# A hand-ordered four-layer graph network kernel: the order of all jobs of a pair, and of the last pairs' jobs, arranged anew

## The chip, the cores and the metric

The kernel runs on one core of one Trainium2 chip. A core has a matmul engine (TensorE, PE in the profile; its weight loads are PEld), a vector engine (DVE), a scalar engine (ACT), GpSimd (POOL), and DMA queues; the kernel issues its transfers from SyncE's queue (SP). Each engine works through its own queue of instructions in the order in which they were emitted and waits where the next one's input or buffer isn't ready. The metric is the device time of one execution in microseconds; lower is better.

## The reference

The input x has 32 batch elements of 512 nodes with 64 features; adj is one 512 x 512 matrix for all. Four layers follow each other, each `x = x + layer(relu(layernorm(x)))`:

```python
# layer 0: v has row 0 set to the intervention value
for _ in range(3):
    effects = adj @ v
    h = relu(concat([v, effects], -1) @ W1.T + b1)
    v = h @ W2.T + b2
# layer 1
for i in range(2):
    z = relu((adj @ z) @ weights[i])
# layer 2: eight heads of gat_layer(x, graph, Wh[k], bh[k]), concatenated, leaky_relu, one gat_layer more, leaky_relu
def gat_layer(x, graph, W, b):
    h = x @ W
    s = einsum('bnd,bmd->bnm', h, h) * graph
    s = where(s == 0.0, -1e16, s)
    return einsum('bnm,bmd->bnd', softmax(s, axis=2), h) + b
# layer 3
h = x @ weight
e = leaky_relu(h @ a[:D] + (h @ a[D:]).T, 0.2)
return softmax(adj_with_unit_diagonal * e, axis=-1) @ h + bias
```

So each batch element needs nine score matrices of 512 x 512 in layer 2 (eight heads and the output layer) and one in layer 3, each with a masked softmax.

## The kernel before

**Pairs and units.** The 32 batch elements are worked as 16 pairs (`NPAIR`), the two elements of a pair side by side in the 128 partitions or along the free axis. The softmax work comes in units of two score matrices. A pair has eight head units: a, b, c, d for its first element (two heads each), g, h, i, j for its second. Unit f holds the output attention of layer 2 of the pair before (class `Out`), and e the attention of layer 3 of the pair before that (class `Last`). The software pipeline thus has several pairs in flight.

**The jobs of a unit.** `begin` takes the tiles. `s0` to `s3` are the scores: for head units and f the matmuls of `gram` (L422 for the product, L425 to add the mask), two PSUM tiles each; in unit e, ACT forms them (L692). `r0` to `r7` are the row maxima with the graph's factor (DVE, L443), and every second one has POOL negate two of them (L450). `x0` to `x3` are two exponentials each (ACT, L454). `nA` and `nB` take a reciprocal (DVE, L464) and four normalisations on POOL (L466). `t0` to `t3` turn the weights in 32 x 32 blocks (DVE, L472).

**The sums.** Two neighbouring units are summed together: number 0 is a with b, 1 is c with d, 3 is g with h, 4 is i with j. `vA` and `vB` (L482, PE) weigh the values, and need all four PSUM tiles of the matmul pool and all eight transposed pieces of both units; `us` copies them out (ACT, L537); `w0`, `w1` apply the head weights (PE, L516), `y0`, `y1` their bias and activation (ACT, L527); `o` is the projection (PE, L545) and `c` its sum over heads (DVE). After the second sum of an element, `f0`/`f1` give the output layer's features HH (PE and ACT), and `h0`/`h1` turn them to nodes: four turns on PE (L588), a copy on ACT to the one buffer `hn`, then sixteen transfers to the values' layout. The joint sum of e and f is number 2: `vA2`, `vB2` (L750), `eu` (ACT, L769 and L771), `er` (turns L588, the residual on DVE, and the output's transfers); then `oA` to `oC` (layer norm before layer 3), `oT`, `oW`, and `oN`, which makes layer 3's values `h3n` (L668) and issues 32 transfers.

**Keys.** `k0`, `k1`, `k3`, `k4` (PE, L798) and `Y0`, `Y1`, `Y3`, `Y4` (ACT, L808) make the left operands of the scores of two head units.

**The front of a pair.** `F0` to `F24` are the steps of the generator `front` (L327): layer norm F0 to F2 (F0 centres and squares on POOL; F1 takes the variance on DVE and its power on POOL, L272; F2 is the product `z` on DVE, L276, its row 0 on DVE, L331, and `xt + b2` on POOL, L332), F3 four turns (L304), F4 to F12 the three steps of layer 0 (F4, F7, F10 node products L324, F5, F8, F11 their sums, F6, F9, F12 the aggregation L312), F13 the residual and the load of x for a later pair, F14 to F16 the next layer norm, F17 to F20 layer 1, F21 to F23 the layer norm before the heads (with copies on POOL, L285), F24 the first element's features `ZZ` and values `ZQ`. `ZZ1` and `ZQ1` are the same for the second element. `values_of` calls `quarters` (L288), which issues sixteen transfers on SP's queue (L294).

**The buffers that couple them.** Scores have four PSUM tiles, all other matmul outputs have four. `hn`, `h3n`, `HH`, `ZZ`, `ZQ` have one buffer each (per element), `Y`, `us` and `z` a few.

**The order.** `manual_schedule` makes the order of emission the order on each engine's queue. It is written by hand into two tables. `PLACES` (L835) gives each job name a tick and a place: a unit that starts in tick t has its job run in tick t + dt, and within a tick the jobs run in the order of their places. A pair has ten ticks (`TICKS`), so in a steady pair the jobs of one tick come from units of different age. `TAIL` (L896) is a list of 160 tokens for the work past the last pair's ten ticks: e and p are the last joint sum's units, r, q and s the output attention and the two layer-3 attentions after it, T, U and E the sums, and 7 the last head unit. `at` looks both up, `place` and `place_sum` name a unit's jobs, and the loop from L957 goes over the pairs:

```python
dt, place = PLACES.get(name, (1, 0))
token = f"{owner[0]}:{name}"
if token in TAIL and (t + dt >= END or owner[0] in list("epqrsEU")):
    dt, place = END + 1 - t, TAIL.index(token)
jobs.setdefault(t + dt, []).append((place, fn))
```

In the last pair the units follow each other in ticks 0 to 7 instead of 0 to 3 and 6 to 9 (`t = base + (i if final else slot)`), so g to j start two ticks sooner there.

Of the kernel before, what the change touches and what calls it, by code (L numbers as in the profile page):

```python
# [21 lines left out]
def gnn_stack_kernel(  # L22
# [77 lines left out]
    E = mybir.EngineType  # L100
# [727 lines left out]
    for n, _ in enumerate(first):  # L828
# [4 lines left out]


    PLACES = {  # L835
        "begina": (0, 98), "s0a": (0, 99), "s1a": (0, 140), "s2a": (0, 203), "s3a": (0, 227),
        "r0a": (0, 118), "r1a": (0, 119), "r2a": (0, 142), "r3a": (0, 165), "r4a": (0, 241),
        "r5a": (0, 260), "r6a": (0, 301), "r7a": (1, 6), "x0a": (0, 237), "x1a": (0, 265), "x2a": (0, 308),
        "x3a": (1, 7), "t0a": (1, 258), "t1a": (1, 149), "t2a": (1, 186), "t3a": (1, 268), "nAa": (1, 83),
        "nBa": (1, 132), "beginb": (-1, 287), "s0b": (-1, 288), "s1b": (-1, 292), "s2b": (0, 65),  # L840
        "s3b": (0, 2), "r0b": (0, 68), "r1b": (0, 86), "r2b": (0, 92), "r3b": (0, 103), "r4b": (0, 163),
        "r5b": (0, 199), "r6b": (0, 107), "r7b": (0, 182), "x0b": (0, 139), "x1b": (0, 128),
        "x2b": (0, 229), "x3b": (0, 208), "t0b": (1, 35), "t1b": (1, 43), "t2b": (1, 45), "t3b": (1, 169),
        "nAb": (0, 212), "nBb": (0, 309), "beginc": (0, 41), "s0c": (0, 42), "s1c": (0, 52),
        "s2c": (0, 188), "s3c": (0, 172), "r0c": (0, 73), "r1c": (0, 75), "r2c": (0, 85), "r3c": (0, 150),
        "r4c": (0, 217), "r5c": (0, 271), "r6c": (0, 240), "r7c": (0, 261), "x0c": (0, 221),
        "x1c": (0, 197), "x2c": (0, 273), "x3c": (0, 269), "t0c": (1, 16), "t1c": (1, 38), "t2c": (1, 54),
        "t3c": (1, 62), "nAc": (0, 276), "nBc": (1, 29), "begind": (0, 47), "s0d": (0, 48), "s1d": (0, 72),
        "s2d": (0, 114), "s3d": (0, 175), "r0d": (0, 80), "r1d": (0, 91), "r2d": (0, 123), "r3d": (0, 131),
        "r4d": (0, 147), "r5d": (0, 179), "r6d": (0, 194), "r7d": (0, 226), "x0d": (0, 148),  # L850
        "x1d": (0, 177), "x2d": (0, 183), "x3d": (0, 234), "t0d": (0, 270), "t1d": (0, 307),
        "t2d": (0, 312), "t3d": (1, 15), "nAd": (0, 247), "nBd": (0, 282), "begine": (0, 21),
        "s0e": (0, 22), "s1e": (0, 23), "s2e": (0, 202), "s3e": (0, 95), "r0e": (0, 138), "r1e": (0, 152),
        "r2e": (0, 159), "r3e": (0, 162), "r4e": (0, 211), "r5e": (0, 230), "r6e": (0, 164),
        "r7e": (0, 181), "x0e": (0, 216), "x1e": (0, 283), "x2e": (1, 70), "x3e": (0, 290), "t0e": (1, 153),
        "t1e": (1, 173), "t2e": (1, 192), "t3e": (1, 228), "nAe": (0, 289), "nBe": (1, 141),
        "beginf": (-1, 25), "s0f": (-1, 311), "s1f": (-1, 26), "s2f": (-1, 313), "s3f": (0, 158),
        "r0f": (0, 27), "r1f": (0, 77), "r2f": (-1, 303), "r3f": (-1, 309), "r4f": (0, 37), "r5f": (0, 90),
        "r6f": (0, 215), "r7f": (0, 254), "x0f": (0, 176), "x1f": (0, 156), "x2f": (0, 280),
        "x3f": (0, 305), "t0f": (0, 274), "t1f": (0, 297), "t2f": (1, 120), "t3f": (1, 124),  # L860
        "nAf": (0, 218), "nBf": (1, 49), "beging": (-1, 299), "s0g": (-1, 300), "s1g": (0, 17),
        "s2g": (0, 109), "s3g": (0, 93), "r0g": (0, 32), "r1g": (0, 64), "r2g": (0, 88), "r3g": (0, 101),
        "r4g": (0, 178), "r5g": (0, 191), "r6g": (0, 129), "r7g": (0, 174), "x0g": (0, 71), "x1g": (0, 121),
        "x2g": (0, 210), "x3g": (0, 209), "t0g": (0, 222), "t1g": (0, 267), "t2g": (1, 61), "t3g": (1, 190),
        "nAg": (0, 220), "nBg": (0, 248), "beginh": (-1, 145), "s0h": (-1, 146), "s1h": (0, 50),
        "s2h": (0, 81), "s3h": (0, 116), "r0h": (0, 78), "r1h": (0, 94), "r2h": (0, 100), "r3h": (0, 108),
        "r4h": (0, 111), "r5h": (0, 115), "r6h": (0, 126), "r7h": (0, 130), "x0h": (0, 134),
        "x1h": (0, 171), "x2h": (0, 180), "x3h": (0, 185), "t0h": (0, 219), "t1h": (0, 296), "t2h": (1, 44),
        "t3h": (1, 87), "nAh": (0, 206), "nBh": (0, 233), "begini": (0, 0), "s0i": (0, 1), "s1i": (0, 10),
        "s2i": (0, 104), "s3i": (0, 67), "r0i": (0, 3), "r1i": (0, 9), "r2i": (0, 20), "r3i": (0, 39),  # L870
        "r4i": (0, 196), "r5i": (0, 200), "r6i": (0, 168), "r7i": (0, 170), "x0i": (0, 79), "x1i": (0, 125),
        "x2i": (0, 243), "x3i": (0, 231), "t0i": (1, 112), "t1i": (2, 89), "t2i": (1, 266), "t3i": (1, 236),
        "nAi": (0, 263), "nBi": (1, 8), "beginj": (-1, 204), "s0j": (-1, 205), "s1j": (-1, 284),
        "s2j": (0, 60), "s3j": (0, 30), "r0j": (-1, 278), "r1j": (0, 4), "r2j": (0, 51), "r3j": (0, 55),
        "r4j": (0, 214), "r5j": (0, 223), "r6j": (0, 117), "r7j": (0, 207), "x0j": (0, 58), "x1j": (0, 102),
        "x2j": (0, 225), "x3j": (0, 253), "t0j": (0, 291), "t1j": (1, 13), "t2j": (1, 96), "t3j": (1, 189),
        "nAj": (0, 262), "nBj": (0, 298), "vA0": (1, 201), "vB0": (1, 279), "us0": (2, 36), "w00": (2, 56),
        "y00": (2, 82), "w10": (2, 105), "y10": (2, 151), "k0": (-1, 242), "Y0": (-1, 259), "vA1": (1, 66),
        "vB1": (1, 306), "us1": (2, 34), "w01": (2, 76), "y01": (2, 97), "w11": (2, 106), "y11": (2, 154),
        "k1": (-1, 193), "Y1": (-1, 235), "vA2": (1, 137), "vB2": (1, 143), "vA3": (1, 110),  # L880
        "vB3": (1, 133), "us3": (1, 251), "w03": (2, 11), "y03": (2, 19), "w13": (2, 40), "y13": (2, 84),
        "k3": (-1, 224), "Y3": (-1, 238), "vA4": (1, 232), "vB4": (1, 256), "us4": (1, 293),
        "w04": (1, 310), "y04": (2, 46), "w14": (2, 53), "y14": (2, 57), "k4": (-1, 295), "Y4": (-1, 302),
        "o01": (2, 244), "c01": (2, 252), "o03": (2, 286), "c03": (3, 127), "f0": (4, 257), "h0": (5, 74),
        "o11": (2, 166), "c11": (2, 272), "o13": (2, 136), "c13": (2, 187), "f1": (3, 33), "h1": (3, 69),
        "eu": (2, 28), "er": (2, 213), "oA": (5, 285), "oB": (5, 294), "oC": (6, 31), "oT": (6, 250),
        "oW": (8, 281), "oN": (9, 12), "ZZ1": (0, 161), "ZQ1": (-1, 157), "F0": (-2, 144), "F1": (-2, 245),
        "F2": (-2, 255), "F3": (-1, 5), "F4": (-1, 155), "F5": (-1, 160), "F6": (0, 14), "F7": (0, 198),
        "F8": (0, 239), "F9": (1, 304), "F10": (2, 135), "F11": (2, 195), "F12": (3, 246), "F13": (4, 18),
        "F14": (4, 59), "F15": (4, 167), "F16": (5, 24), "F17": (5, 277), "F18": (6, 63), "F19": (7, 249),  # L890
        "F20": (7, 264), "F21": (7, 275), "F22": (8, 122), "F23": (8, 184), "F24": (9, 113),
    }

    TAIL = """  # L896
        7:t2j e:begine e:s0e p:beginf p:s2f 7:t3j e:s1e e:r0e e:r2e e:s2e p:s1f e:r4e e:r5e e:s3e T:vA4 T:vB4
        e:x2e p:s0f T:us4 T:w04 e:r6e e:r3e e:r7e p:r4f T:y04 p:r5f p:r0f p:r2f T:w14 e:x3e e:r1e p:s3f p:r3f
        e:nBe p:r1f T:y14 p:x1f p:r6f e:x0e U:f0 p:x0f T:o13 T:c13 p:r7f T:f1 p:nAf e:t3e p:x2f r:beginf r:s0f
        r:r0f r:r1f T:h1 p:x3f r:s2f p:t1f e:t2e p:nBf e:x1e r:r4f e:nAe 7:x3j r:r5f r:x0f U:h0 r:s3f p:t2f  # L900
        r:r6f r:r7f e:t0e p:t3f p:t0f r:x3f r:s1f e:t1e r:r2f r:r3f E:vA2 r:x2f E:vB2 r:x1f 7:nBj r:nBf r:nAf
        r:t0f r:t1f E:eu r:t2f r:t3f E:er E:oA E:oB r:vA5 E:oC r:vB5 r:ou E:oT r:or E:oW E:oN q:begine q:s0e
        q:s2e q:r0e q:r1e q:s1e q:r2e r:oA r:oB q:r4e q:s3e r:oC q:r3e r:oT q:r6e r:oW q:r7e q:x1e q:x0e q:r5e
        r:oN s:begine s:s0e s:s3e s:r0e q:x3e q:x2e q:nAe s:s1e s:s2e s:r1e s:r6e s:r7e s:x3e q:t1e q:nBe
        s:r2e s:r3e q:t0e s:r4e s:r5e q:t2e s:x0e s:x2e s:nBe s:x1e q:t3e s:nAe s:t2e q:vA5 q:vB5 s:t3e s:t0e
        q:lu s:t1e q:lr s:vA5 s:vB5 s:lu s:lr
    """.split()
    PER_SUM = ("us", "w0", "y0", "w1", "y1")
    jobs = {}
    LEAD, TICKS = 2, 2 * NQ + 2  # L910
    END = LEAD + TICKS * NPAIR - 2
    owner = [None]

    def at(t, name, fn):
# [126 lines left out]
```

## Time and profile before

| what | us |
|---|---|
| the three runs | 2363.77, 2368.61, 2368.47 (median 2368.47) |
| the profiled execution's own time | 2365.83 |
| its span, from the first to the last instruction | 2364.0 |
| start, 0 to 160 | 160, PE busy 120.2 |
| first steady pair's run-up, 160 to 297.15 | 137.2, PE busy 134.2 |
| 13 steady pairs, 297.15 to 2098.76 | 1801.6, PE busy 1753.0 |
| last pair, 2098.76 to 2235 | 136.2, PE busy 125.3 |
| the rest, 2235 to 2364 | 129.0, PE busy 71.4 |

Busy time of the whole span: PE 2204.1 us (93%), DVE 1880.1 (80%), ACT 1500.4 (63%), POOL 1301.3 (55%). The mean granted clock of TensorE is 0.981 of full speed. A pair's beginning is taken at the first of the four aggregations on `z` (L312). The costliest groups of instructions, with their count and mean length, are

| line, engine, operation | count | mean ns |
|---|---|---|
| L454 ACT exponential, 128x512 | 1280 | 718 |
| L466 POOL normalisation, 128x512 | 1280 | 703 |
| L472 DVE transpose, 128x1024 | 640 | 1229 |
| L443 DVE maximum, 128x512 from PSUM or SBUF | 1152 | 681 |
| L422 PE scores, 64x512 | 4096 | 603 |
| L482 PE weighted sums, 32x256 | 17152 | 374 |
| L272 POOL power, 128x8 | 64 | 1739 |

In a row of the timeline the columns are: begin in us, length, engine, line, operation, output and inputs, shapes, count, and in brackets the idle time before it and what ended that. A matmul row joins the matmuls that follow each other without a gap on one line.

### The profile page before, as it was taken

How to read it: one execution, taken by the hardware profiler on the slowest of the kernel's cores; microseconds unless marked ns; L12 is line 12 of the kernel's file. 1: busy time of each engine (PE TensorE's matmuls, PEld its weight loads, DVE VectorE, ACT ScalarE, POOL GpSimd, SP SyncE). 2: the span in 40 equal slices, each digit the busy share in tenths (PEclk: the TensorE clock that was granted, in tenths of full speed). 3: DMA queues.
4: the chain of work that ended last, by engine and by line, in shares of the span. 5: the costliest groups of instructions: out<-in, count | busy, mean ns of one | idle time of the engine just before them, and what ended most of it. 6: DMA issues, size and time to landing. Idle time of an engine off the chain costs nothing.

```text
span 2364.0 us, 81802 instructions
## 1 busy us (share of the span) xinstructions
PE 2204.1 (93%) x34507; PEld 1194.3 (51%) x34507; DVE 1880.1 (80%) x4098; ACT 1500.4 (63%) x3752; POOL 1301.3 (55%) x2163
## 2 busy tenths in 40 slices
PE   6889999999999999999999999999999999998873
PEld 3445555555555555555555555555555555554442
DVE  3668788888888888888888888878888888888754
ACT  1446557666675766767676666757666675766644
POOL 2345565645655565556566556656555655555433
PEclk9999999999999999999999999999999999999986
DMA  3101011111111111111111111111111111111112
GB/s 85 19 6 31 13 25 32 30 21 31 31 28 28 32 31 21 31 31 30 26 33 32 21 29 31 32 25 33 30 24 29 30 28 25 30 27 26 20 25 46
DMA packets 260596, 68.25 MB, mean 29 GB/s; under 512 B 257660, under 2 KB 258692, under 8 KB 260228
## 3 DMA queue, kind: packets, MB, share of 16 engines
q1 hardware_dynamic: 259424, 62.86, 15.8%
q8 instruction: 270, 4.42, 0.8%
q14 instruction: 98, 0.80, 0.1%
q10 hardware_dynamic: 804, 0.17, 0.0%
HBM read 8.40 MB, written 4.19 MB: 5 GB/s over the span
## 4 chain that ended last, share of the span: by engine, by line
PE 71%; DVE 11%; ACT 6%; POOL 5%; issue 2%; SPq 2%; DMA 2%; ACTq 0%; POOLq 0%; DVEq 0%
PE s L422 18%; PE mm L482 14%; PE mm L312 9%; PE mm L750 6%; DVE sm L472 4%; PE mm L516 4%; PE s L425 4%; DVE sm L443 4%; PE mm L545 3%; PE mm L324 3%; ACT sm L454 3%; POOL sm L466 3%; SPq L294 2%; PE mm L798 2%; PE mm L358 2%
## 5 line engine op out<-in xcount | busy, mean ns | idle before, releaser
L454 ACT ACTIVATE sm<-sm,nmx 128x512 f32<-128x512 f32 x1280 | 909.2, 718 | 184.4 <-POOL nmx L450 180.9
L466 POOL TENSOR_SCALAR sm<-sm,rs 128x512 f32<-128x512 f32 x1280 | 874.4, 703 | 213.3 <-DVE rs L464 206.5
L472 DVE STREAM_TRANSPOSE sm<-sm 128x1024 f32<-128x1024 f32 x640 | 775.2, 1229 | 92.3 <-POOL sm L466 86.1
L443 DVE CUSTOM_DVE_ANT_0 sm<-s,A 128x512 f32<-128x512 f32 x1152 | 732.5, 681 | 134.4 <-PE s L425 127.0
L422 PE MATMUL s<-ZZ,Y 64*64 64x512 f32 x4096 | 571.4, 603 | 25.7 <-ACT Y L808 18.5
L482 PE MATMUL mm<-sm,vq 32*64 32x256 f32 (+1 forms) x17152 | 487.8, 374 | 22.8 <-DVE sm L472 18.9
L450 POOL TENSOR_SCALAR nmx<-mx 128x2 f32<-128x2 f32 x640 | 147.4, 234 | 614.9 <-DVE mx L443 555.4
L482 PEld LDWEIGHTS mm<-sm,vq 32*64 32x64 f32 x17152 | 397.0, 133 | 125.4 <-issue 45.3
L422 PEld LDWEIGHTS s<-ZZ,Y 64*64 64x64 f32 x4096 | 152.7, 132 | 248.7 <-issue 119.0
L425 PE MATMUL s<-NEGM,I2b 64*64 64x512 bf16 x2304 | 261.4, 377 | 0.0
L454 ACT ACTIVATION_READ_ACCUMULATOR sm<-sm,nmx 128x1 f32 x1280 | 248.9, 194 | 0.0
L537 ACT COPY us<-mm 128x256 f32<-128x256 f32 x256 | 75.8, 378 | 166.9 <-PE mm L482 166.9
L527 ACT ACTIVATE y<-mm,cols 128x512 f32<-128x512 f32 x256 | 158.3, 689 | 30.2 <-PE mm L516 30.2
L312 PE MATMUL mm<-AT,v 128*128 128x512 f32 x384 | 173.0, 593 | 0.0
L750 PE MATMUL mm<-sm,vq 32*64 32x128 f32 (+1 forms) x5504 | 133.1, 315 | 33.7 <-issue 17.1
L425 PEld LDWEIGHTS <-I2b 64*64 64x64 bf16 x2304 | 83.1, 107 | 158.3 <-issue 157.5
L272 POOL TENSOR_TENSOR r<-ve,mhalf 128x8 f32<-128x8 f32 x64 | 111.3, 1739 | 76.7 <-DVE ve L270 61.1
L750 PEld LDWEIGHTS mm<-sm,vq 32*64 32x64 f32 x5504 | 114.0, 133 | 59.4 <-issue 30.8
L516 PE MATMUL mm<-us,Wh 64*64 64x512 f32 x1024 | 132.7, 595 | 0.7 <-ACT us L537 0.7
L545 PE MATMUL mm<-y,Wo_sb 128*64 128x512 f32 x512 | 124.5, 605 | 0.0
L312 PE MATMUL mm<-AT,z 128*128 128x512 f32 x256 | 118.8, 607 | 2.0 <-DVE z L276 1.4
L312 PEld LDWEIGHTS mm<-AT,v 128*128 128x128 f32 x384 | 73.1, 191 | 92.8 <-issue 91.2
(135 smaller groups left out, 1987.2 us busy)
## 6 DMA issues: line engine op xcount, KB each, us to landing
vq<-z SPq DMA_DIRECT2D x512, 32.0 KB, 1.9
vq<-hn SPq DMA_DIRECT2D x512, 32.0 KB, 1.9
vq<-h3n SPq DMA_DIRECT2D x512, 32.0 KB, 1.9
xt<-in_x_dram SPq DMA_DIRECT2D x32, 128.0 KB, 2.5
out_dram<-xo SPq DMA_DIRECT2D x32, 128.0 KB, 2.1
A<-in_adj_dram SPq DMA_DIRECT2D x3, 1024.0 KB
Wh<-in_L_gnn_Wh_dram SPq DMA_DIRECT2D x2, 256.0 KB
Wo_sb<-in_L_gnn_W_out_dram SPq DMA_DIRECT2D x1, 256.0 KB
```

The costliest lines, as they stand in the source:

```text
L312: nc.tensor.matmul(pe, lhsT=v[:, m].rearrange("p j d -> p (j d)"), rhs=AT[:, m, :], start=(first and m == 0), stop=(m == NT - 1),)
L422: nc.tensor.matmul(pss[half][R[ab], :], lhsT=lhsT, rhs=rhs, start=True, stop=False)
L425: nc.tensor.matmul(pss[half][R[ab], :], lhsT=I2b[R[half], :], rhs=NEGM[R[half], k, :], start=False, stop=True,)
L443: nc.vector.tensor_tensor_reduce(self.sm[:, s, :], src, graph, 1.0, -FMAX, ALU.mult, ALU.max, self.mx[:, s : s + 1])
L454: nc.scalar.activation(self.sm[:, s, :], self.sm[:, s, :], AF.Exp, bias=self.nmx[:, s : s + 1], accum_out=self.ssum[:, s : s + 1],)
L466: nc.gpsimd.tensor_scalar(self.sm[:, s, :], self.sm[:, s, :], self.rs[:, s : s + 1], 1.0, ALU.mult, ALU.mult)
L472: nc.vector.transpose(out=two, in_=two)
L482: nc.tensor.matmul(self.u[i][R[c], 0 : weights.shape[1] * 32], lhsT=values[32 * i : 32 * i + 32, jb, :], rhs=weights[32 * i : 32 * i + 32, ...
L516: nc.tensor.matmul(py[c][r, :], lhsT=Wh2[R[c], 2 * (self.q - 1 + c) + ab, r], rhs=self.us[R[c], 2 * ab : 2 * ab + 2].rearrange("p i (s e) ...
L527: nc.scalar.activation(y, py[c], AF.Prelu, bias=cols[:, h : h + 1], alpha=0.01)
L545: nc.tensor.matmul(pa[R[ab], :], lhsT=Wo_sb[:, h, :], rhs=self.y[h], start=(k == 0), stop=(k == 1),)
L750: nc.tensor.matmul(self.u[i][R[c], (s % NS) * 32 : (s + ns) * 32], lhsT=values(i)[r, jb, :], rhs=sm[r, s : s + ns, 32 * jb : 32 * jb + 32] ...
```

## The change

Only the two tables are changed. 312 of the 315 names in `PLACES` get another tick or place, and the 160 tokens of `TAIL`, the same ones, stand in another order. No job is added, taken out or altered, nor are the tiles, the buffers or the code that reads the tables. What an engine's queue holds in a pair is the same; the order differs, and for some jobs the pair period in which they run.

Cut to the entries that the prediction speaks of (each name's tick and place; the numbers are only ranks, so that two entries compare only within one table):

```diff
     PLACES = {
...
-        "s2i": (0, 104), "s3i": (0, 67), "r0i": (0, 3), "r1i": (0, 9), "r2i": (0, 20), "r3i": (0, 39),
+        "s2i": (0, 63), "s3i": (0, 68), "r0i": (0, 25), "r1i": (0, 29), "r2i": (0, 51), "r3i": (0, 56),
...
-        "k4": (-1, 295), "Y4": (-1, 302), "f0": (4, 257), "h0": (5, 74), "begini": (0, 0), "s0i": (0, 1),
+        "k4": (-1, 265), "Y4": (-1, 312), "f0": (4, 259), "h0": (5, 3), "begini": (0, 8), "s0i": (0, 9),
...
-        "t1h": (0, 296), "t2h": (1, 44), "t3h": (1, 87), "F20": (7, 264), "F21": (7, 275), "F22": (8, 122),
+        "t1h": (0, 248), "t2h": (0, 282), "t3h": (1, 59), "F20": (7, 260), "F21": (7, 292), "F22": (8, 72),
...
-        "F0": (-2, 144), "F1": (-2, 245), "F2": (-2, 255), "F3": (-1, 5), "nAi": (0, 263),
+        "F0": (-2, 84), "F1": (-2, 241), "F2": (-2, 258), "F3": (-1, 32), "nAi": (0, 249),
...
-        "us1": (2, 34), "w01": (2, 76), "y01": (2, 97), "s2f": (-1, 313), "s3f": (0, 158),
+        "us1": (1, 293), "w01": (2, 6), "y01": (2, 50), "s2f": (0, 77), "s3f": (0, 76),
...
-        "nBe": (1, 141), "r5f": (0, 90), "x2f": (0, 280), "x3f": (0, 305), "nBf": (1, 49), "t3f": (1, 124),
+        "nBe": (1, 128), "r5f": (0, 170), "x2f": (0, 250), "x3f": (0, 291), "nBf": (1, 2), "t3f": (1, 62),
...
-        "t0c": (1, 16), "t1c": (1, 38), "t2c": (1, 54), "t3c": (1, 62), "r5c": (0, 271), "r7d": (0, 226),
+        "t0c": (0, 311), "t1c": (0, 244), "t2c": (1, 160), "t3c": (1, 184), "r5c": (0, 245), "r7d": (0, 179),
...
-        "k1": (-1, 193), "Y1": (-1, 235), "o13": (2, 136), "F8": (0, 239), "t3j": (1, 189),
+        "k1": (-1, 125), "Y1": (-1, 164), "o13": (2, 185), "F8": (0, 178), "t3j": (1, 193),
...
-        "ZQ1": (-1, 157), "F24": (9, 113), "oN": (9, 12), "h1": (3, 69),
+        "ZQ1": (5, 281), "F24": (9, 209), "oN": (9, 12), "h1": (3, 48),
...
     TAIL = """
-        7:t2j e:begine e:s0e p:beginf p:s2f 7:t3j e:s1e e:r0e e:r2e e:s2e p:s1f e:r4e e:r5e e:s3e T:vA4 T:vB4
-        e:x2e p:s0f T:us4 T:w04 e:r6e e:r3e e:r7e p:r4f T:y04 p:r5f p:r0f p:r2f T:w14 e:x3e e:r1e p:s3f p:r3f
-        e:nBe p:r1f T:y14 p:x1f p:r6f e:x0e U:f0 p:x0f T:o13 T:c13 p:r7f T:f1 p:nAf e:t3e p:x2f r:beginf r:s0f
...
+        e:begine e:s0e 7:t2j e:s3e 7:t3j p:beginf p:s0f e:s2e T:vA4 e:r4e e:s1e T:vB4 p:s2f e:r5e e:r2e T:us4
+        e:r3e p:r0f e:r6e e:x1e p:r1f T:w04 e:r7e p:r4f T:y04 p:r5f p:s1f T:w14 e:r0e e:x2e p:r2f T:y14 p:s3f
+        e:r1e e:x3e e:x0e e:nBe T:o13 T:c13 p:r3f U:f0 T:f1 p:x0f e:nAe e:t2e e:t3e e:t0e T:h1 p:r6f p:x2f
...
```

In words, as they fall out on the queues of a steady pair:

- `h0` stands after `k4` and before the scores of i, instead of among them; t1 and t2 of h stand before F20's and F21's DVE instructions.
- F2 stands after i's first normalisation; before, i's came after it.
- `w01` stands right behind f's first scores, ahead of the scores s3 and s2 of f; before it stood behind s2. `us1` moves with it to the tick before.
- f's x2 stands before `eT`, and its r5 behind e's second normalisation.
- c's t1 stands before its r5 and t0, its t2 and t3 behind d's maxima; j's t3 behind F8; `k1` before `o13`.
- `ZQ1`'s sixteen transfers stood right behind F24's sixteen of the same pair, at the end of the pair period; now they stand in the next period, behind those of `h1`, of `oN` and the load of x, five ticks after the pair begins.
- In `TAIL` the sum of i and j stands right behind the first scores of e and f, and the jobs from `o13` to `h1` stand earlier.

## The prediction, on record before the changed kernel was run

> **What bounds the kernel now.** I read the page first, then the busy time in windows of one pair each, the timeline of TensorE over one pair, and the other engines' timelines wherever TensorE stood.
>
> ```profile
> span 2364.0 us, 81802 instructions
> ...
> PE   6889999999999999999999999999999999998873
> ...
> PEclk9999999999999999999999999999999999999986
> ```
>
> After a start of some 150 us the matmul engine is nine tenths busy or more at full clock; only the last 130 us are loose. A pair repeats at the line "L312 x8 on z"; the windows between two such places are these (span of the window, then PE, PEld, DVE, ACT and POOL busy, the clock, the DMA share and GB/s):
>
> ```profile
> 297.15:435.34 138.19, 134.62 (x2146) 73.19 (x2145) 116.28 (x254) 92.83 (x233) 81.13 (x134) 1.00 0.16 27
> ...
> 989.74:1128.03 138.29, 134.80 (x2146) 73.00 (x2145) 117.05 (x256) 93.61 (x235) 81.12 (x134) 1.00 0.17 29
> ...
> 2235.00:2364.00 129.00, 71.41 (x1584) 46.67 (x1584) 65.42 (x139) 59.05 (x146) 46.83 (x71) 0.75 0.19 32
> ```
>
> The mean of the 13 pairs between 297.15 and 2098.76 is 138.59 us, of which TensorE works 134.8. DVE at 117 has 21 us to spare, ACT and POOL more. No job is added or removed, so a pair can gain only what TensorE stands, 3.5 us, plus what is hidden in stretched groups. The timeline of TensorE in the pair from 989.74 shows where it stands:
>
> ```profile
> 996.78 1.09 PE L422 MATMUL s<-ZZ,Y 64*64 64x512 f32 x8 [0.69 <-ACT Y L808]
> ...
> 1013.45 0.63 PE L304 MATMUL mm<-ident,z 128*128 128x128 f32 x4 [1.02 <-DVE rs L464]
> ...
> 1093.91 1.35 PE L422 MATMUL s<-HH 64*64 64x512 f32 x6
> ...
> 1112.00 4.73 PE L750 MATMUL mm<-sm,vq 32*64 32x256 f32 x210 [0.80 <-DVE sm L472]
> ```
>
> First the scores of unit i wait for Y4; then F3's turns wait (the named reciprocal is only the last DVE event, the real supplier is z of F2 and its row 0, L331, written at 1013.09); the scores f s2 are stretched by two maxima that still hold their PSUM tiles; then the joint sum waits for the last transpose of f. The DVE and POOL timelines give the cause of the second:
>
> ```profile
> 1009.60 1.67 POOL L272 TENSOR_TENSOR r<-ve,mhalf 128x8 f32<-128x8 f32 x1
> 1011.23 1.27 POOL L332 TENSOR_TENSOR xt<-xt,b2bc 128x512 f32<-128x512 f32 x1
> ...
> 1011.30 1.75 DVE L276 SCALAR_TENSOR_TENSOR z<-xc,r 128x512 f32<-128x512 f32 x1 [1.79 <-POOL r L272]
> ```
>
> z takes 1.75 us beside POOL's xt+b2; elsewhere in this pair its shortest is 0.69.
>
> **The change part by part.** It moves the place of 312 of 315 job names and reorders the tail list. Most moves leave a job between the same neighbours on TensorE; I cost those that touch a stand or make one, with the durations above.
>
> *h0 between k4 and the scores of i.* Before, k4 (ends 996.09), Y4 on ACT (its first half ends 996.74), s0 of i. Now h0's four turns, 0.60 us in the row at 1000.70, fill 0.60 of the 0.69. The later place of h0 is emptied: i s0 to s3 follow each other, held only by DVE's maxima r0 to r3, which end at 1000.56 as before. On DVE transposes t1 and t2 of h move ahead of F20 and F21, into the 1.14 us in which DVE waited for F20, so one transpose (1.15) leaves the stretch before F22. The sum of g and h, at 1002.53 before, starts at about 1001.8, and its own stretch (7.52 against 7.09 in its other places, it waited for h t3) goes as well. Gain 0.7 to 1.1, taken 0.9.
>
> *F0 to F3.* From F22's first DVE instruction to F3 it took 10.60 us (1002.85 to 1013.45), in a chain DVE–POOL–DVE–POOL–DVE: variance, power (1.67), z, centring (1.04), square (1.04), variance, power, z. TensorE has 7.09 of sum and 2.4 of scores over it. F2 now stands behind i nA, so POOL normalises i (L466) beside z, and xt+b2 comes after it. At 1094.38 z beside L466 took 0.69; so 1.06 leaves the chain, which becomes 9.5 and just fits under 9.5. Gain 1.0; bounds 0 (z stays at 1.75) and 1.06. Row 1094.38 is the same instruction beside the same POOL instruction, so I take its price.
> The Trainium skill (SBUF — State Buffer, Who interferes with whom) speaks against this: a DVE instruction with two SBUF inputs and a GpSimd instruction that reads SBUF block each other, and the second to issue waits for the first. By it z could wait for one normalisation of 0.68, and the gain would be about 0.4, the sum some 8 us smaller; the row at 1094.38 shows no such wait.
>
> *w01 ahead of f s2.* Now TensorE meets w01 right after f s0 (ends 1093.9), and w01 needs us1, the third ACT job after e x1. In ACT's queue e x3 stands before us1, and its bias, POOL's L450, stands behind the power of F15 (it ended at 1093.44). With F15 one maximum (0.61) earlier e x3 starts at about 1092.9, us1 at 1094.3, w01 at 1095.0: a new stand of 1.1. Behind it wait f s3, f s2, w11, k3 and through them Y3. In return f s2 is no longer stretched (1.88 instead of 1.08, so 0.8). Net loss 0.3; bounds 0 (us1 as early as POOL allows) and 1.3 (us1 at 1095.12 as now).
>
> *The joint sum.* f x2 moves before eT and f r5 behind e nB's normalisation on POOL, but the last chain (f x3, f nB, 2.71 of POOL, f t3) keeps its order; worked through, f t3 ends at 1111.4 instead of 1111.95, and TensorE, 0.3 later, gets there at 1111.5. Gain 0 to 0.8, taken 0.3.
>
> *The other moves.* c t1 goes ahead of c r5 and t0, c t2 and t3 behind d's maxima, j t3 behind F8, k1 before o13. Each costs DVE, ACT or POOL the same instructions; what hides them is 7.09 of TensorE per head sum. I put them at nothing; if the cover of the c–d stretch is gone, it is the last rival below.
>
> *ZQ1.* Its 16 transfers on SP's queue move from the end of the previous pair's jobs to behind h1, oN's 32 and the load of xt. In a steady pair these are issued by 1107.1; 16 at 0.645 and 1.95 to land end at 1119.4, 21 us before the sum that reads them: nothing. In the last pair, units g to j come two ticks sooner, and there it counts:
>
> ```profile
> 2186.00 23.76 SPq L294 DMA_DIRECT2D vq<-h3n  x32
> ```
>
> By this row SP is free at 2209.8, the 13th of 16 (at 0.74, as in this row) lands at 2221, the last at 2223. That sum ran from 2215.28 and ended at 2224.0; now its first quarter runs as the pieces land and three quarters of 7.1 follow: 2228. Loss 4, and the gains of k1 and k4 in the last pair (their Y waits of 2.08 and 1.58) are lost in this stand. Bounds 0 and 8.
> The skill (TensorE: Matmul & The Clock Gate, Part 1) says that a matmul engine idle for about 3.4 us falls to half clock; by that the sum after this stand would need up to 3.5 more. In the trace the clock was 0.83 and a sum took 8.54 instead of 7.09 after stands of 2.87 and 0.98.
>
> *The tail list.* The sum of i and j now stands before f's scores s1 and s2, so it starts when j t3 is turned (2240.3) and not at 2242.35: 2 less. From its end to h1's copy I count 12.5 us in the new order, against 14.2, since two or three exponentials less stand before f1's copy on ACT. From that copy on SP sets the end (16 issues, landing, second copy, joint sum at 2277.73; then twice 32 issues), as before. Gain 3.5 against the loss of 4.
>
> Sum: 0.9 + 1.0 − 0.3 + 0.3 = 1.9, rounded to 2.0 with the small shortenings, in 14 pairs (0 to 13) is 28; 0.7 in pair 14, which has no F3; tail −0.5. From 2365.8 of the profiled execution: **2338 us**. Its time lies 2.6 below the median of the runs shown (2368.47) and within them.
>
> **The rivals.**
> *More is gained:* the stand before the joint sum (0.80+0.33+0.66) goes too and w01 does not wait: 3.7 a pair, 14 times, 52 less: 2314. For it: DVE has 21 us of slack a pair. Against: f nB's chain keeps its order.
> *The gain is eaten:* w01 waits 1.3, z stays slow and the joint sum slips by as much as TensorE came early; the order of nearly all TensorE jobs is the same, so the pair stays 138.6: 2366, between 2358 and 2371. For it: all these supplies come from queues that were on time by under 1 us.
> *Slower:* c t1 waits in DVE's queue for POOL's fourth normalisation (2.71 instead of the 1.59 that t0 waited), and c t2 and t3 (2.3) now lie behind d's maxima, before the sum of c and d. DVE would be late there by 1.1 + 2.3 = 3.4, less the 2.0 gained: 1.4 a pair, 14 times: 2386. It decides once DVE's idle time between 1065.3 and the sum at 1085.68, 2.8 us in its timeline, is used up by these; most of that idle time waits for POOL and ACT, which move too.
>
> **How the numbers follow.** Forecast 0.47 (own range 2326 to 2354), more 0.15, eaten 0.18, slower 0.20. A measurement of this kernel can tell 0.2% (4.7 us) from no change. Of "eaten", 0.06 is still faster, 0.10 within, 0.02 above. Faster 0.68, same 0.10, slower 0.22. The range 2312 to 2375 takes in the first three and leaves out most of the fourth.
>
> **What would show it.** Right: a pair of 136 to 137 us; the first scores of i within 0.2 us of h0; z in F2 near 0.7 and no stand before F3; in the last pair a stand of several us before the sum of g and h. Wrong in its step: z at 1.75; w01 standing over 1.3 us; the sum of c and d waiting for a transpose. The prediction as a whole is wrong if the pair stays above 138.

## The result and the profile after

The changed kernel takes 2348.24 us (median of four runs, 2346.53 to 2349.57) beside 2367.72 for the kernel before: a ratio of 0.9921, with a 95% interval of 0.9903 to 0.9938. The forecast was 2338 in a range of 2312 to 2375. The profiled execution took 2346.53 with a span of 2344.7, 19.3 less than before.

From the page of the changed kernel (span; then PE's busy tenths and its granted clock in 40 slices):

```profile
span 2344.7 us, 81823 instructions
...
PE   6889999999999999999999999999999999999883
...
PEclk9899999999999999999999999999999999999986
```

The windows of the changed kernel (span, then busy time of PE, PEld, DVE, ACT, POOL, the clock, DMA share and GB/s) have the start, the pair that answers to the one shown of before, all 13 steady pairs, and the rest:

```profile
160.00:301.10 141.10, 135.23 (x1894) 70.99 (x1895) 108.87 (x240) 82.53 (x211) 72.92 (x127) 0.96 0.11 19
...
985.64:1122.04 136.40, 133.19 (x2147) 71.99 (x2145) 116.53 (x256) 93.34 (x235) 81.64 (x134) 1.00 0.17 29
...
301.10:2078.71 1777.61, 1733.10 (x27874) 937.63 (x27873) 1514.03 (x3314) 1212.89 (x3041) 1061.28 (x1742) 1.00 0.17 29
...
2215.00:2344.70 129.70, 78.08 (x1601) 51.52 (x1600) 69.17 (x143) 61.87 (x154) 47.35 (x74) 0.74 0.19 32
```

A pair now takes 136.74 us instead of 138.59 (1777.61 / 13), so the 13 steady pairs give 24.0, more than the 19.3 by which the span fell. Of that 4.8 were given back: the first marker (F19's aggregation, the row "L312 on z") stands at 301.10 instead of 296.99, 4.1 later, and what follows the last marker takes 266.04 instead of 265.35, 0.7 more.

The timeline of TensorE in the pair from 985.64 has the places that were shown of before:

```profile
992.08 0.66 PE L588 MATMUL mm<-ident,HH 128*128 128x128 f32 x4
992.84 1.09 PE L422 MATMUL s<-ZZ,Y 64*64 64x512 f32 x8
...
997.98 7.16 PE L482 MATMUL mm<-sm,vq 32*64 32x256 f32 x256
...
1007.46 0.63 PE L304 MATMUL mm<-ident,z 128*128 128x128 f32 x4
...
1089.14 1.09 PE L516 MATMUL mm<-us,Wh 64*64 64x512 f32 x8 [1.30 <-ACT us L537]
...
1105.94 4.67 PE L750 MATMUL mm<-sm,vq 32*64 32x256 f32 x201 [0.28 <-DVE sm L472]
```

The first four rows have no brackets: h0's turns fill the wait for Y4, the sum of g and h runs in one piece, and F3 finds its z. The fifth is a new stand (idle time of TensorE), w01 waiting for us1. The last is the old wait before the joint sum, 0.28 instead of 0.80.

To compare kernels, the pair is cut at fixed rows of TensorE's timeline, from the beginning of one to the beginning of the next, and averaged over the 13 steady pairs of each profiled execution. Only the stretches that differ are shown; the runs are explained below.

| run | marker to sum gh | sum gh | its end to w03 (F3 within) | end of sum cd to F17 | F17 to joint sum | joint sum | whole pair | first marker at | after last marker |
|---|---|---|---|---|---|---|---|---|---|
| before | 12.95 | 7.53 | 3.95 | 7.12 | 12.08 | 9.93 | 138.59 | 297.0 | 265.4 |
| changed | 12.34 | 7.10 | 2.94 | 7.67 | 11.72 | 10.33 | 136.74 | 301.1 | 266.0 |
| F2 alone | 12.95 | 7.53 | 3.18 | 7.10 | 12.06 | 10.22 | 138.32 | 297.1 | 266.8 |
| h0 alone | 12.35 | 8.13 | 3.94 | 7.09 | 12.06 | 10.11 | 138.73 | 295.8 | 267.5 |
| h0, t1, t2 | 12.35 | 7.12 | 3.83 | 7.06 | 12.06 | 10.17 | 137.68 | 295.7 | 267.1 |
| w01 alone | 12.95 | 7.55 | 3.92 | 8.00 | 12.21 | 10.18 | 139.85 | 295.3 | 268.9 |
| list alone | 12.95 | 7.53 | 3.94 | 7.10 | 12.06 | 10.07 | 138.71 | 296.8 | 262.5 |
| four places, list | 12.35 | 7.17 | 3.04 | 7.10 | 12.06 | 10.15 | 137.13 | 295.8 | 260.8 |
| changed, w01 back | 12.34 | 7.16 | 2.93 | 8.96 | 11.71 | 10.28 | 138.08 | 300.9 | 269.3 |
| changed, ZQ1 early | 12.36 | 7.15 | 2.94 | 7.62 | 11.71 | 10.25 | 136.92 | 300.4 | 260.6 |
| changed, g t3 late | 12.34 | 7.16 | 2.93 | 7.70 | 11.71 | 10.44 | 136.96 | 298.3 | 267.3 |
| both of these | 12.36 | 7.15 | 2.94 | 7.69 | 11.71 | 10.39 | 137.04 | 297.4 | 260.1 |
| and f moved | 12.36 | 7.09 | 2.95 | 6.91 | 12.17 | 10.20 | 136.52 | 296.5 | 261.6 |

Kernels with one and the same steady order (the changed one, and those with ZQ1 or g's t3 moved) differ by up to 0.3 in the pair, so smaller differences of that column say nothing. The execution of before that was profiled took 2365.83, 2.6 below the median shown ahead (2368.47), and its joint sum is the shortest here: with the same steady order the list alone has 10.07 and a pair of 138.71.

### The profile page after: what moved, and what is told of

The parts are those of the page before. It is cut to its first block, busy times and chain, and to the rows that moved or that the text cites. A ratio compares the mean times of both kernels' runs of the same rounds, so it can differ in the third digit from the quotient of the medians.

```text
span 2344.7 us, 81823 instructions
## 1 busy us (share of the span) xinstructions
PE 2189.2 (93%) x34507; PEld 1186.5 (51%) x34507; DVE 1872.8 (80%) x4098; ACT 1496.4 (64%) x3752; POOL 1306.7 (56%) x2163
## 4 chain that ended last, share of the span: by engine, by line
PE 76%; DVE 10%; ACT 6%; POOL 3%; issue 2%; SPq 2%; DMA 1%; ACTq 0%; POOLq 0%; DVEq 0%
PE s L422 19%; PE mm L482 16%; PE mm L312 11%; PE mm L750 5%; PE mm L545 5%; PE s L425 4%; PE mm L516 4%; DVE sm L443 4%; DVE sm L472 4%; ACT sm L454 3%; PE mm L324 3%; PE mm L798 2%; SPq L294 2%; PE mm L358 2%; ACT y L527 1%
## 5 line engine op out<-in xcount | busy, mean ns | idle before, releaser
L482 PE MATMUL mm<-sm,vq 32*64 32x256 f32 (+1 forms) x17152 | 488.1, 378 | 29.8 <-DVE sm L472 20.3
L482 PEld LDWEIGHTS mm<-sm,vq 32*64 32x64 f32 x17152 | 400.3, 135 | 129.3 <-issue 56.6
L312 PE MATMUL mm<-AT,v 128*128 128x512 f32 x384 | 172.9, 593 | 0.0
L750 PE MATMUL mm<-sm,vq 32*64 32x128 f32 (+1 forms) x5504 | 131.4, 313 | 27.4 <-issue 21.5
L750 PEld LDWEIGHTS mm<-sm,vq 32*64 32x64 f32 x5504 | 111.8, 132 | 52.7 <-issue 29.4
L263 POOL TENSOR_TENSOR xc<-x,nmu 128x512 f32<-128x512 f32 x48 | 55.3, 1151 | 139.8 <-DVE nmu L261 139.8
L312 PE MATMUL mm<-AT,z 128*128 128x512 f32 x256 | 119.1, 609 | 3.8 <-DVE z L276 1.4
```

The lines of the kernel that those rows point to most:

```text
L312: nc.tensor.matmul(pe, lhsT=v[:, m].rearrange("p j d -> p (j d)"), rhs=AT[:, m, :], start=(first and m == 0), stop=(m == NT - 1),)
L482: nc.tensor.matmul(self.u[i][R[c], 0 : weights.shape[1] * 32], lhsT=values[32 * i : 32 * i + 32, jb, :], rhs=weights[32 * i : 32 * i + 32, ...
L750: nc.tensor.matmul(self.u[i][R[c], (s % NS) * 32 : (s + ns) * 32], lhsT=values(i)[r, jb, :], rhs=sm[r, s : s + ns, 32 * jb : 32 * jb + 32] ...
```

## The experiments

Each says from which of the two kernels it starts; edits are shown as entries of the tables. Ratios are to the kernel before, timed beside each of them.

### F2 alone, in the kernel before

```diff
-        "F2": (-2, 255),
+        "F2": (-2, 263.5),
```

> The kernel before with one move: F2 behind i's first normalisation, so that z lies beside POOL's normalisations and xt + b2 comes after. Theory (contention with the addition on POOL stretched z): z falls from 1.75 to about 0.7 us, the stand before F3 of 1.0 goes, 14 pairs give 14 us: about 2353.5. Rival (z waits for one normalisation of 0.68 instead): z about 1.4 with its wait, 0.4 a pair, about 2362. Rival (F3 was not what held the pair, the next supply is as late): no change, 2367.

Measured: 2362.93 us, ratio 0.9967 (0.9955 to 0.9980): half of what was expected. POOL's and DVE's timelines of this run at F2:

```profile
1009.93 3.23 POOL L466 TENSOR_SCALAR sm<-sm,rs 128x512 f32<-128x512 f32 x4
1013.13 1.28 POOL L332 TENSOR_TENSOR xt<-xt,b2bc 128x512 f32<-128x512 f32 x1
...
1009.98 0.69 DVE L276 SCALAR_TENSOR_TENSOR z<-xc,r 128x512 f32<-128x512 f32 x1 [1.72 <-POOL r L272]
1010.70 0.52 DVE L331 COPY z<-ivt 1x128 f32<-1x128 f32 x1
```

z takes 0.69 as in the theory, and the rival with z at 1.4 is out. The two engines still get in each other's way, but in other places: the four normalisations take 3.23 instead of 2.71 (the first 1.21), and the copy of row 0 behind z, which F3 needs too, is longer than in the kernel before:

```profile
1013.09 0.21 DVE L331 COPY z<-ivt 1x128 f32<-1x128 f32 x1
```

From the begin of z to the end of row 0 it takes 1.25 instead of 2.01 (means of the 13 pairs), so 0.76 leaves the chain and not 1.06, and the stretch with F3 falls by 0.77. A wait of 0.25 for row 0 remains in this pair, since F22 comes no earlier: it begins 0.33 after the sum of g and h, as in the kernel before, and 0.20 ahead of it in the changed kernel. Of the 0.77, the pair keeps 0.27; 0.20 comes back before the sum of i and j, and the joint sum is 0.29 longer.

### h0 alone, and h0 with two transposes, in the kernel before

```diff
-        "h0": (5, 74),
+        "h0": (5, -1),
```

> The kernel before with one move: h0 ahead of the scores of i. Theory: the wait for Y4 (0.69) is filled, but the sum of g and h still waits for h t3, whose DVE queue is unchanged, so that its stretch grows by what it starts earlier: 0 to 0.3 a pair, 2363 to 2368. Rival (the filler alone makes the gain that the forecast put at 0.6 of its 0.9): 0.6 a pair, 2359.

Measured: 2369.93 us, ratio 0.9998 (0.9988 to 1.0007), no change. The sum of g and h begins 0.60 earlier and takes 0.60 longer. The timeline of TensorE in that run shows what it meets:

```profile
1002.10 0.66 PE L482 MATMUL mm<-sm,vq 32*64 32x256 f32 x8
1003.16 7.14 PE L482 MATMUL mm<-sm,vq 32*64 32x256 f32 x248 [0.40 <-DVE sm L472]
```

Eight matmuls run, then the sum waits for h's last transpose: the filler moved the stand and removed nothing. The second run also puts h's t1 and t2 ahead of F20 and F21 on DVE:

```diff
-        "h0": (5, 74), "t1h": (0, 296), "t2h": (1, 44),
+        "h0": (5, -1), "t1h": (0, 263.5), "t2h": (0, 274.5),
```

> As the run with h0 ahead of the scores of i, and h's transposes t1 and t2 ahead of the DVE instructions of F20 and F21. Theory (h t3 was the limit, and comes 1.15 earlier by this): the sum of g and h starts 0.6 earlier and takes 7.09 instead of 7.52, together 1.04 a pair as in the changed kernel, 14 pairs: about 2353. Rival (the other moves of the changed kernel were needed for it): under 0.5 a pair, over 2360.

Measured: 2354.44 us, ratio 0.9931 (0.9916 to 0.9946), with 12.35 and 7.12 in the table as in the changed kernel. With no other move these three bring 1.01 of the 1.04 that the two stretches gain in the changed kernel. The filler needs the transposes; the transposes without the filler were not run.

### The list of the last pairs alone

The kernel before, with all 160 tokens of `TAIL` in the changed kernel's order:

```diff
-        7:t2j e:begine e:s0e p:beginf p:s2f 7:t3j e:s1e e:r0e e:r2e e:s2e p:s1f e:r4e e:r5e e:s3e T:vA4 T:vB4
...
+        e:begine e:s0e 7:t2j e:s3e 7:t3j p:beginf p:s0f e:s2e T:vA4 e:r4e e:s1e T:vB4 p:s2f e:r5e e:r2e T:us4
...
```

> The kernel before with the new list of the last pairs' jobs alone. Theory (the list is worth what the forecast said): 3.5 less, about 2364, all of it behind the last pair's period. Rival (SP's 64 issues of the last two groups of h3n set the end, and they start only a little earlier): under 1.5 less, 2366 to 2368.

Measured: 2364.43 us, ratio 0.9977 (0.9967 to 0.9987), 5.4 less; in the profile 262.5 after the last marker, where the kernels with the old list and the old ZQ1 have 265.4 to 268.9. By these rows the list is worth 3 to 6. The rival's limit of 1.5 less lies outside the interval, so it is out.

### ZQ1's transfers early in the changed kernel

```diff
-        "ZQ1": (5, 281),
+        "ZQ1": (0, 231),
```

The timelines of TensorE and of SP's queue in the last pair of the changed kernel show the stand that this is to remove:

```profile
2193.91 0.65 PE L482 MATMUL mm<-sm,vq 32*64 32x256 f32 x4
2195.75 0.61 PE L482 MATMUL mm<-sm,vq 32*64 32x256 f32 x2 [1.19 <-DMA vq<-z]
2198.33 8.50 PE L482 MATMUL mm<-sm,vq 32*64 32x256 f32 x250 [1.97 <-DMA vq<-z]
...
2166.15 22.30 SPq L294 DMA_DIRECT2D vq<-h3n  x32
2188.54 10.25 SPq L294 DMA_DIRECT2D vq<-z  x16
```

SP is busy with h3n until 2188.5, ZQ1's first pieces are issued then, the last at 2198.8, and the sum takes 12.85 from its first matmul to the next scores instead of 8.71 before. Part of that is the clock: the last 250 matmuls take 8.50 at a granted clock of 0.83, where 250 took 7.15 at 1.00 in the kernel before.

> The changed kernel with one move: ZQ1's sixteen transfers right behind the sum of the pair before that reads the old values, instead of behind those of h1 and oN. Theory: the waits for vq of 1.19 and 1.97 in the last pair's sum of g and h go and that sum takes 7.1 to 8 us instead of 12.85; some 4 us there, of which the later waits give back at most half: 2344 to 2346. Rival (the end is set by SP's 64 issues of the last h3n, which start when the layer norms are done whatever came before): under 1 less, 2347.5. In the steady pairs both expect nothing: 136.7.

Measured: 2342.47 us, ratio 0.9880 (0.9865 to 0.9895), clear of the changed kernel's 0.9921. The same sum in this run:

```profile
2195.69 7.66 PE L482 MATMUL mm<-sm,vq 32*64 32x256 f32 x256
```

There is no wait, and what follows the last marker is 5.4 shorter (260.6 beside 266.0). The theory let later waits give back up to half of the gain; the whole of it reached the end.

### w01 back in the changed kernel, and w01 alone in the kernel before

```diff
-        "w01": (2, 6), "y01": (2, 50),
+        "w01": (2, 77.5), "y01": (2, 78),
```

> The changed kernel with one move undone: w01 (and y01) behind f's scores s3 and s2. Theory (the stand of 1.30 before w01 is new, and the scores stretched by 0.8 were the smaller evil): 0.5 a pair less, 14 pairs 7 us: about 2341. Rival (the scores are held by their maxima as before and the joint sum waits for f's last transpose anyway): no change, 2348.

Measured: 2369.01 us, ratio 0.9994 (0.9985 to 1.0004): the whole gain is gone, and both the theory and the rival are wrong. The timelines of TensorE and ACT in this run:

```profile
1096.55 0.59 PE L516 MATMUL mm<-us,Wh 64*64 64x512 f32 x2
...
1101.02 1.55 PE L312 MATMUL mm<-AT,z 128*128 128x512 f32 x3 [0.89 <-ACT y L527]
...
1097.68 1.30 ACT L527 ACTIVATE y<-mm,cols 128x512 f32<-128x512 f32 x2 [1.13 <-PE mm L516]
1098.88 0.71 ACT L454 ACTIVATE sm<-sm,nmx 128x512 f32<-128x512 f32 x1
1099.59 0.71 ACT L454 ACTIVATE sm<-sm,nmx 128x512 f32<-128x512 f32 x1
1100.29 1.25 ACT L527 ACTIVATE y<-mm,cols 128x512 f32<-128x512 f32 x2
```

ACT stands 1.13 for w01, then does y01, f's x1 and y11; F17 waits for the PSUM tile that y11 gives back. The changed kernel has f's x1 between y01 and y11, so by these rows a late w01 delays F17 by the exponentials too. The reverse question is what w01 ahead does in the old order, where y01 and y11 are neighbours on ACT:

```diff
-        "w01": (2, 76), "s2f": (-1, 313),
+        "w01": (2, 34.5), "s2f": (0, 36),
```

> The kernel before with w01 ahead of f's scores s2 alone. Theory (w01 has to wait for us1 on ACT wherever it stands, and whatever is put behind it waits too; that undoing it in the changed kernel cost 1.3 a pair comes from y11 and f's x1 having been put around it on ACT): the stretch from the sum of c and d to F17 grows from 7.12 to between 7.6 and 8.1, of which the wait before the joint sum, 0.8, can take up to 0.8: 0 to 0.5 a pair, 2369 to 2376. Rival (w01 early is worth 1.3 a pair by itself, as its undoing cost): 2351.

Measured: 2387.77 us, ratio 1.0074 (1.0057 to 1.0091): slower, on the theory's side but by more than its 0.5 a pair. The stretch grows to 8.00, within its bounds, and the wait before the joint sum absorbs none of it (0.94 instead of 0.80). The row of w01 in this run:

```profile
1101.70 1.09 PE L516 MATMUL mm<-us,Wh 64*64 64x512 f32 x8 [1.71 <-ACT us L537]
```

So the place of w01 has no price of its own. In the old order it costs 1.26 a pair to put it early (0.88 of it in this stretch, 0.25 in a longer joint sum), in the new one 1.34 to put it late. That the order on ACT makes the difference is argued from the two traces; no run changed that order alone.

### g's t3 behind h's r3 in the changed kernel

In the start of the changed kernel, the scores before F19 wait 7.32 us (5.02 before). DVE's timeline there:

```profile
159.38 1.25 DVE L472 STREAM_TRANSPOSE sm<-sm 128x1024 f32<-128x1024 f32 x1
160.84 2.58 DVE L472 STREAM_TRANSPOSE sm<-sm 128x1024 f32<-128x1024 f32 x2 [0.21 <-POOL sm L466]
163.34 0.65 DVE L443 CUSTOM_DVE_ANT_0 sm<-s,A 128x512 f32<-128x512 f32 x1
```

The maximum that frees the scores' PSUM tile stands behind four transposes, one more than before.

```diff
-        "t3g": (1, 40),
+        "t3g": (1, 104),
```

> The changed kernel with one move undone: g's transpose t3 behind h's maximum r3. Theory (in the first pair, which has no e and f between, DVE's maxima of h stand behind two transposes that wait for POOL, the stand of 7.32 at 164 us): about 1.2 us less in the start alone, nothing in the steady pairs: 2347. Rival (the start lost its time elsewhere, to the order of i and the granted clock): no change in the start; with t3 later the sum of g and h may wait for it in every pair, 2348 to 2356.

Measured: 2349.16 us, ratio 0.9908 (0.9893 to 0.9923), not told from the changed kernel's 0.9921. In the profile the wait is 5.99 instead of 7.32 and the first marker comes at 298.3 instead of 301.1. So t3's place makes 1.3 of the 2.3 by which this wait had grown; its effect on the time of the whole is below what these runs resolve.

### Four places and the list, in the kernel before

```diff
-        "F2": (-2, 255), "h0": (5, 74), "t1h": (0, 296), "t2h": (1, 44),
+        "F2": (-2, 263.5), "h0": (5, -1), "t1h": (0, 263.5), "t2h": (0, 274.5),
```

and `TAIL` as changed.

> The kernel before with h0, h's t1 and t2, and F2 moved as in the changed kernel, and the new list of the last pairs' jobs: four places and the list, the other 308 places as they were. Theory (these carry the gain of the changed kernel): 1.0 a pair at the sum of g and h, 0.75 at F3, and 5 at the end, less 0.3 a pair of longer joint sums: a pair of 137.1 to 137.4, about 2345 in all, as fast as the changed kernel. Rival (the gains at F3 and at the sum need the reordered work of f behind them, else the joint sum waits for f's last transpose longer): the wait before the joint sum grows from 0.8 to over 1.5, a pair of 138, 2352 or more.

Measured: 2340.93 us, ratio 0.9883 (0.9868 to 0.9898), faster than the changed kernel and than expected. The pair is 137.13, and the wait before the joint sum stays as it was:

```profile
1102.43 4.74 PE L750 MATMUL mm<-sm,vq 32*64 32x256 f32 x210 [0.79 <-DVE sm L472]
```

The other 308 places bring 0.39 a pair (5.1 in 13), hardly more than the differences that say nothing, and cost 5.3 before the first marker and 5.2 behind the last. ZQ1 is one of these places, and by the run above it alone accounts for the 5.2.

### Both repairs of the changed kernel, and three moves of f

```diff
-        "ZQ1": (5, 281), "t3g": (1, 40),
+        "ZQ1": (0, 231), "t3g": (1, 104),
```

> The changed kernel with ZQ1 right behind the sum that frees its buffer and g's t3 behind h's r3, the two moves that were tried alone. Theory (one acts in the last pair, the other in the first): the gains add, 6 and 2, about 2340 beside 2348; the first pair's marker at 298.3 instead of 301.1, no wait for vq before the sum of g and h of the last pair. Rival (the start's gain is lost again before the steady pairs, as the time of the run with t3 alone may say): 2342.5.

Measured: 2338.42 us, ratio 0.9870 (0.9854 to 0.9887). The first marker is at 297.4 and what follows the last takes 260.1, as expected of each; beside the run with ZQ1 alone the intervals overlap. The next kernel moves three jobs of f besides:

```diff
-        "s3f": (0, 76), "w11": (2, 100), "y11": (2, 127), "r7f": (0, 221),
+        "s3f": (0, 5), "w11": (2, 79), "y11": (2, 80), "r7f": (0, 210),
```

> The kernel with ZQ1 and g's t3 moved, and besides: f's scores s3 ahead of w01, y11 ahead of f's exponentials x1, f's maximum r7 ahead of its first normalisation. Theory (w01 waits for us1 on ACT anyway, s3 fits into that stand of 1.30; F17 waits for y11's PSUM tile and not for matmuls; the last exponential of f waits for the negation behind POOL's normalisations): the stretch from the sum of c and d to F17 falls from 7.67 to between 6.6 and 7.1, the wait before the joint sum stays under 0.8, a pair gains 0.4 to 0.9, 6 to 12 us, some 2331. Rival (ACT has no idle time in this stretch and sets the joint sum): the stretch falls but the wait before the joint sum grows by as much, no change beside the run without these moves.

Measured: 2335.11 us (2334.17 to 2336.4), ratio 0.9858 (0.9843 to 0.9872), the fastest here; all its runs lie below all of the one before it (2337.61 to 2340.78). The gain is 3.3, not the 6 to 12 expected. The theory's first half holds: the stretch to F17 falls from 7.69 to 6.91. Of these 0.78, the next stretch takes 0.46 back, but not as the rival had it: the wait before the joint sum is gone, and the scores of g before it are slower. TensorE and DVE in this run:

```profile
1095.12 1.32 PE L422 MATMUL s<-ZZ,Y 64*64 64x512 f32 x6
...
1091.90 2.58 DVE L472 STREAM_TRANSPOSE sm<-sm 128x1024 f32<-128x1024 f32 x2 [0.45 <-POOL sm L466]
1094.40 0.65 DVE L443 CUSTOM_DVE_ANT_0 sm<-s,A 128x512 f32<-128x512 f32 x1
```

The scores need a tile that the maximum at 1094.40 frees, and this stands behind two transposes that wait for POOL's normalisation. From the end of the sum of c and d it comes 14.13 later (mean of the 13 pairs), in the changed kernel 13.87: TensorE came early, and this supply didn't.

## Why the prediction was right

The direction, the mechanism of the main gain and the range were right; the size was two thirds of the forecast (19.5 of 30 by the medians). Four places with the list, moved alone, bring as much and more, so the cause of the gain is shown. Point by point:

- **The pair:** 1.85 less, forecast 1.9 to 2.0. That it fits so well is in part luck: w01 and the joint sum fell short by 0.6 together, and h0 and the small moves, put at nothing, made up for 0.5. *h0* was put at 0.9 and measured 1.04 in the changed kernel, 1.01 with three places alone. The forecast named both halves, but its 0.6 for the filler is worth nothing without h's transposes (h0 alone: 0.9998).
- **F0 to F3** was put at 1.0 and gives 1.01 in the changed kernel, but not by z alone. z takes 0.69 as the row at 1094.38 had it, and all 14 of before that took 1.75 or more are gone (13 other products of this line now take 0.96 instead of 0.69); the copy of row 0 behind it, which the step didn't price, grew from 0.21 to 0.52, so the move itself gives 0.77, and 0.27 in the pair. With h0, t1 and t2 besides, which bring F22 forward, the stretch falls by 0.91. The Trainium skill (SBUF — State Buffer, Who interferes with whom) says that the order of issue decides who blocks. By the begins in the profile POOL was first both times: beside xt + b2, 0.07 ahead, z took 1.75, as the rule has it; beside the normalisations, 0.04 ahead, z lost nothing and POOL's four took 0.51 longer, which doesn't agree, unless the order of issue was another than these begins show.
- **w01** was put at a loss of 0.3 and lost 0.55, within its bounds, with a stand of 1.30 for the forecast's 1.1, at the edge of what it named as a sign of being wrong. The step priced TensorE's order and ACT's up to us1, and left out what ACT does behind it, which by the traces is why undoing it doesn't give the loss back but costs 1.3.
- **The joint sum** was put at a gain of 0.3 and gave none: 0.36 less ahead of it, where the wait fell from 0.80 to 0.28, and 0.40 more in it, from pauses that no wait explains. Part of the 0.40 is the short joint sum of the profiled execution of before (9.93, where the other runs with the old steady order have 10.07 to 10.22). The small moves, put at nothing, gave 0.4 in sum.
- **The number of pairs** is the first step that failed: "in 14 pairs (0 to 13) is 28" takes the start as unchanged and its last part as a steady pair. The aggregation of F19 before the first marker comes at 169.13 instead of 164.11, so 5.0 are lost where nothing was forecast, and from there to the first marker 0.9 is won and not 2. In pair 0, which has no e and f, DVE's transposes of g hold up h's maxima and so the scores; moving g's t3 back wins about 2.8 of this in the trace. The rest isn't settled.
- **The end:** ZQ1 was put at a loss of 4. The stand came where the forecast put it, the sum grew by 4.1, and taking the stand out won 5.4. The lower clock, for which the prediction named up to 3.5, cost this sum 1.4. The list was put at 3.5 and is worth 3 to 6. Both mechanisms were right, with sizes off by 1 to 2. Sum: 0.7 lost after the last marker where 0.2 was to be won (0.7 in pair 14 less 0.5).
- **The rivals:** the wait of c's transposes before the sum of c and d, named as the way to a slower kernel, doesn't appear: that sum takes 7.12 and 7.11, and from the end of the sum ahead of it to its begin it takes 0.11 less. Of the other two, neither the pair of 138.6 nor the joint sum without any wait came about.

So from the profiled times, 28.2 forecast less 19.3 measured leaves 8.9: 6.1 up to the first marker, 2.0 in the 13 pairs, and 0.9 at the end, but for rounding.

## What to carry to other kernels

Filling a stand on the bounding engine gains nothing if the next wait behind it keeps its supply, so try the filler and the supply together. The price of a job's place on one engine can turn round with the order of the rest, so price it within the order that it will stand in. An order tuned on the steady state should be priced apart in the first and last periods, where other work is in flight: here they cost the changed kernel 10 us beside the kernel with four of its 312 places and the list, which did better than all 312.

## What the runs showed of the hardware

The joint sum (L750, 384 small matmuls with as many weight loads) pauses in most pairs twice, 128 of its matmuls apart, for 0.2 to 1.5 us each, with no wait that the profile can name. In the 13 steady pairs of the changed kernel its length varies from 9.84 to 11.72, and the mean of these pauses was 1.24 a pair before and 1.62 after, though the same instructions run.

The pauses have no fixed place in the sum: the first moves on by 24 to 26 matmuls from pair to pair. Counted in all records of PE's queue (matmuls, weight loads, waits), the 26 pauses in the steady pairs of before lie exact multiples of 256 records apart. The head sums (L482), with a matmul every 27 ns where the joint sum has one every 22 ns between its pauses, show no such pause in the steady pairs. In the list of the DMA queues of before, one queue carries instructions:

```profile
q8 instruction: 270, 4.42, 0.8%
```

These are 270 packets of 16,384 bytes, and PE's queue has 69,243 records, 270 times 256 and a rest. Each of the 26 pauses ends 1.2 to 1.6 us after one of these packets has landed; the 13 waits before the joint sum end 3.6 to 15.1 us after one. So by the trace the pauses look like TensorE waiting for its next 256 instructions. No run changed anything about it, so this is not shown by experiment, nor why the pauses differ between executions.
